# Rare blocks moved into open products, the next expert's rows fetched ahead of the overflow block, and one turn moved by six products

## The chip, the core and the metric

The kernel runs on one core of a Trainium2 chip. The metric is the device time of one execution in microseconds. The engines are PE (TensorE, matmuls and transposes through the array), DVE (VectorE), ACT (ScalarE), POOL (GpSimd) and SP (SyncE, which here issues the weight loads). Each engine works through its own queue in order, and engines wait for one another through semaphores.

## The reference

The reference is one layer of a graph network on N = 625 nodes with D = 1024 features and 20000 edges, all in float32:

```python
xn = _layernorm(x)
x = x + sage_twice(xn, src, dst) + linear_attention(xn)
x = x + moe(_layernorm(x))

# sage layer:   mean = segment_sum(h[src], dst) * deg_inv
#               h @ W_self + mean @ W_neigh + b          (relu between the two)
# attention:    softmax(q, over d) * 64**-0.5, softmax(k, over n); (q @ (k^T v)) @ Wo + bo   (16 heads of 64)
# moe:          softmax router over 8 experts, the best 2 of each node:
#               sum_k top_k * (silu(x @ w1[e_k]) @ w2[e_k])
#               + sigmoid(x @ sgw) * ((silu(x @ gate) * (x @ up)) @ sdown)
```

## The kernel before

**How a product is made.** Matmuls run on numbers split into a high half (a copy to float32r) and a low half (the rest), so that a product of x and w is three matmuls: high by high, high by low, low by high. A weight arrives in chunks of 128x1024 through a `Stream`: SP loads `wraw` (or `wmore`, further buffers in the expert stage), ACT casts it to `whi`, DVE subtracts to get `wlo` (both in the helper `split`, L99). There are three buffers each of `whi` and `wlo`, so the two engines run up to about two chunks ahead of PE. The stream's order is the order in which the weights were added at the start. `ts_half` (L201) is the product of all 625 rows by half of a weight's columns: four chunks `u`, in each of them five row tiles of six matmuls, into five banks of PSUM that stay open over the four chunks. A `step(u)` can be called after each chunk.

**The stages around the change, in order.** `psc` (L742) makes the attention context. Then comes the first rare block, `recount`, in a `tc.If(rare_v > 0)` (L748): it is for an adjacency count that does not fit the packed form, and with the inputs given it is not taken; the branch itself is executed by every engine. `psa` (L759) applies the context, `pso` (`ts_half` at L771) is the product with Wo, whose result is added to x on DVE and stored in DRAM (`accd`, L780) by POOL. `neighbours(xn)` (L783) is the first layer's product with W_neigh: `psg`, its tiles split into `g0h` and `g0l`. The second rare block (L793) follows, then `psag` (L819), the sums over neighbours. The second layer has the same form: `neighbours`, then `psx` (L847) with the self weights, added to `x2` (loaded back from `accd`, L851), the third rare block (L853), and `last_mean` (`psm`, L874), the sums over neighbours for the five tiles of rows in two groups, (0, 1, 2) and (3, 4). Where an If is not taken, an engine waits for its own work before it and then branches; an engine that needs a result or a buffer from another engine on the far side waits for that engine's branch.

**The second layer norm.** After a tile's means are complete, DVE adds them to `x2` and takes the statistics, ACT writes the normalised tile `xfn` (L273), and `turn` (L865) transposes it: eight PE transposes into two `pst` banks (L284), split by ACT and DVE into `xfh` and `xfl`. Tile 0 is turned inside tile 3's products, tiles 1 and 2 after tile 3, tile 3 and 4 inside the first products of the shared expert (`psga`, `psup`, L222).

**The experts.** Tokens are scattered by expert into `xsd`. Eight experts are taken by rank of load (`RANKS` = 0, 1, 2, 6, 3, 4, 5, 7), with room for 224, 224, 224, 128, 160, 160, 160, 128 rows in that order. Six are wide (`expert_wide`, L1178), two of 128 rows narrow. In a wide expert the first product (`pse`, L1196 and L1200) takes `xs`, the turned rows, through w1 in eight chunks; two `set` copies and additions (L1205, L1206), a silu and a split give `he`; the second product (`psy`, L1230 and L1253 to L1255) takes `he` through w2 in eight chunks, two halves of four; `y` is copied out and stored in `ysd` by POOL.

The rows of an expert come through a `Turn` (L1000). Making it issues the loads of `xb` on POOL (`expert_load`, L988; there is one buffer, so the turns of the expert before must have read it). Each `step()` finishes the turn before it (ACT copies the high half to `xs`, POOL subtracts the low half, both L99) and starts another: a 32x32 block transposition on DVE (`raw`, L1031). A wide expert has four turns. They are spread over the second product of the expert ahead:

```python
                if half or u > 1:
                    nxt().step()
...
                if aside and (half, u) == (0, 0):
                    aside(accs)
```

`aside` is `overflow` (L1292), for the first expert alone: a block for rows beyond an expert's room. It is not taken with these inputs. `nxt()` makes the Turn when it is first called.

## Time and profile before

| what | value |
|---|---|
| median of three runs | 1013.51 us (1012.4 to 1014.13) |
| the profiled execution | 1012.98 us |
| its span in the profile | 1011.4 us |
| PE busy | 996.1 us, 98%, 5541 instructions |
| DVE, ACT, POOL busy | 598.1, 395.3, 149.1 us |
| granted TensorE clock, mean over the span | 0.997 |

A time in the text such as "709" is in microseconds from the start of the span. In the list of waits, a line gives the engine, the tile it writes and the line of code, then what ended the wait, then the microseconds in total, how often, and the longest. In the chain of waits, the first two columns are start and length; "issue" is time in which the engine waits for nothing that the profile shows. In the table of windows, each engine has its busy time and number of instructions, then come the granted TensorE clock, the share of the DMA engines and GB/s. A releaser with a q (DVEq, PEq) is an engine's sequencer, here at a branch.

### The profile page before, as it was taken

What the parts mean: (1) busy time and instruction counts of PE and PEld (TensorE: products, weight loads), DVE (VectorE), ACT (ScalarE), POOL (GpSimd) and SP (SyncE); (2) the same over time, 40 slices, a digit from 0 to 9 for tenths busy, and PEclk for the clock granted to TensorE, in tenths of its full rate; (3) what the DMA queues carried; (4) which work ended last, traced back from release to release, by engine and by line L of the source; (5) the groups of instructions that cost most, each with busy time, mean ns of one, the idle gap of its engine ahead of it and who ended that gap; (6) DMA issues with size and microseconds to landing.
All of it is one profiled execution on the core that took longest, in us unless ns stands there. A gap on an engine that the chain in (4) does not pass through costs nothing. (4 is left out here: it accounts for less than half of the span.)

```text
span 1011.4 us, 14754 instructions
## 1 busy us (share of the span) xinstructions
PE 996.1 (98%) x5541; PEld 861.1 (85%) x5541; DVE 598.1 (59%) x1213; ACT 395.3 (39%) x577; POOL 149.1 (15%) x206
## 2 busy tenths in 40 slices
PE   9999999999999999999999999999899999999998
PEld 6999998888888888888878999997879787887886
DVE  7998745672523226333247264366777788887681
ACT  5534242231311122122116242264647576766610
POOL 1000011210145000200001003301332203120030
PEclk9999999999999999999999999999999999999999
DMA  8122237672234321412220226667877897887871
GB/s 243 53 64 67 81 117 257 229 246 73 96 122 155 124 84 43 143 63 83 84 63 3 64 63 208 204 188 228 238 240 238 276 348 248 282 299 252 333 257 53
DMA packets 111464, 164.67 MB, mean 163 GB/s; under 512 B 5931, under 2 KB 63443, under 8 KB 111382
## 3 DMA queue, kind: packets, MB, share of 16 engines
q1 hardware_dynamic: 97734, 118.38, 36.1%
q0 software_dynamic: 13456, 45.08, 13.6%
q8 instruction: 46, 0.75, 0.3%
q14 instruction: 36, 0.29, 0.1%
q10 hardware_dynamic: 192, 0.16, 0.0%
HBM read 133.19 MB, written 30.42 MB: 162 GB/s over the span
## 5 line engine op out<-in xcount | busy, mean ns | idle before, releaser
L99 DVE TENSOR_TENSOR wlo<-wraw,whi 128x1024 fp32r<-128x1024 f32 x148 | 186.4, 1260 | 249.1 <-ACT whi L99 244.8
L99 ACT CAST whi<-wraw 128x1024 fp32r<-128x1024 f32 x148 | 155.5, 1051 | 277.5 <-PE psg L212 66.2
L1200 PE MATMUL pse<-xs,whi 128*128 128x448 f32 (+1 forms) x384 | 110.9, 361 | 2.8 <-POOL xs L99 2.8
L99 DVE TENSOR_TENSOR wlo<-wmore,whi 128x1024 fp32r<-128x1024 f32 x67 | 82.2, 1227 | 28.2 <-ACT whi L99 27.0
L1196 PE MATMUL pse<-xs,wlo 128*128 128x224 f32 (+1 forms) x384 | 90.1, 255 | 0.0
L99 ACT CAST whi<-wmore 128x1024 fp32r<-128x1024 f32 x67 | 70.4, 1050 | 43.8 <-PE psz L212 17.0
L401 PE MATMUL psk<-xnh,whi 128*128 128x384 f32 (+3 forms) x240 | 74.5, 312 | 0.3 <-ACT xnh L99 0.3
L1200 PEld LDWEIGHTS pse<-xs,whi 128*128 128x128 f32 x384 | 69.9, 191 | 5.8 <-POOL xs L99 3.3
L402 PE MATMUL psk<-xnl,whi 128*128 128x384 f32 (+3 forms) x240 | 73.5, 306 | 0.6 <-DVE xnl L99 0.6
L403 PE MATMUL psk<-xnh,wlo 128*128 128x384 f32 (+3 forms) x240 | 73.5, 306 | 0.0
L1196 PEld LDWEIGHTS pse<-xs,wlo 128*128 128x128 f32 x384 | 72.8, 192 | 0.8
L1253 PE MATMUL psy<-whi,he 128*128 128x512 f32 (+1 forms) x176 | 69.5, 395 | 0.7 <-PEq L1295 0.7
L1254 PE MATMUL psy<-wlo,he 128*128 128x512 f32 (+1 forms) x176 | 69.6, 395 | 0.3 <-DVE wlo L99 0.2
L1255 PE MATMUL psy<-whi,he 128*128 128x512 f32 (+1 forms) x176 | 69.0, 392 | 0.0
L484 DVE TENSOR_SCALAR hot<-iota,srow,unit 125x128 f16<-125x128 f16 x160 | 49.4, 309 | 0.0
L402 PEld LDWEIGHTS psk<-xnl,whi 128*128 128x128 f32 x240 | 45.5, 190 | 0.8 <-DVE xnl L99 0.8
L401 PEld LDWEIGHTS psk<-xnh,whi 128*128 128x128 f32 x240 | 45.4, 190 | 0.6 <-ACT xnh L99 0.6
L403 PEld LDWEIGHTS psk<-xnh,wlo 128*128 128x128 f32 x240 | 45.4, 189 | 0.0
L99 POOL TENSOR_TENSOR xs<-raw,xs 128x512 fp32r<-128x512 f32 (+2 forms) x24 | 32.6, 1375 | 84.8 <-ACT xs L99 72.1
L483 DVE TENSOR_SCALAR hot<-iota,edt 125x128 f16<-125x128 f16 x160 | 39.6, 249 | 4.1 <-PE pa L501 4.1
L1253 PEld LDWEIGHTS psy<-whi,he 128*128 128x128 f32 (+1 forms) x176 | 31.9, 181 | 10.9 <-ACTq L1295 1.1
L1254 PEld LDWEIGHTS psy<-wlo,he 128*128 128x128 f32 (+1 forms) x176 | 31.8, 180 | 10.0 <-DVE wlo L99 1.6
(354 smaller groups left out, 2360.4 us busy)
## 6 DMA issues: line engine op xcount, KB each, us to landing
wraw<-in_L_ffn_w_dram SPq DMA_DIRECT2D x65, 512.0 KB, 5.3
wmore<-in_L_ffn_w_dram SPq DMA_DIRECT2D x63, 512.0 KB, 5.2
xsd<-zt POOLq DMA_DIRECT2D x9, 1024.0 KB, 5.5
wraw<-in_L_gnn_W_self_dram SPq DMA_DIRECT2D x16, 512.0 KB, 3.6
wraw<-in_L_gnn_W_neigh_dram SPq DMA_DIRECT2D x16, 512.0 KB, 3.7
wraw<-_ffn_shared_gate_up_dram SPq DMA_DIRECT2D x16, 512.0 KB, 3.9
wraw<-in_L_mix_Wk_dram SPq DMA_DIRECT2D x8, 512.0 KB, 6.1
wraw<-in_L_mix_Wq_dram SPq DMA_DIRECT2D x8, 512.0 KB, 3.7
```

The source lines that it names most:

```text
L99: return (order(nc.scalar.copy(hi, srcap)), order((eng or nc.vector).tensor_sub(lo, srcap, hi.bitcast(F32))))
L401: nc.tensor.matmul(ps[:, :n], wh[:, kt, :], xnh[:, kt, c], start=kt == 0, stop=False)
L402: nc.tensor.matmul(ps[:, :n], wh[:, kt, :], xnl[:, kt, c], start=False, stop=False)
L403: nc.tensor.matmul(ps[:, :n], wl[:, kt, :], xnh[:, kt, c], start=False, stop=kt == KT - 1)
L483: nc.vector.tensor_scalar(h[:ET, :WIN], iota[:ET, :WIN], edst[e], None, op0=ALU.is_equal)
L484: return nc.vector.tensor_scalar(h[:ET, WIN:], iota[:ET, :WIN], srow[e], unit[e].bitcast(F32), op0=ALU.is_equal, op1=ALU.mult)
L1196: nc.tensor.matmul(ps[a][:, :n], wl[:, k, c], xs[:, kt, 0, :], start=False, stop=False)
L1200: nc.tensor.matmul(ps[a][:, :2 * n], wh[:, k, c], xs[:, kt], start=kt == 0, stop=kt == KT - 1)
L1253: nc.tensor.matmul(acc, h(kt, 0), wh[:, k, :], start=kt == 0, stop=False)
L1254: nc.tensor.matmul(acc, h(kt, 0), wl[:, k, :], start=False, stop=False)
L1255: nc.tensor.matmul(acc, h(kt, 1), wh[:, k, :], start=False, stop=kt == KT - 1)
```

## The change

1. `neighbours(xn)` with its `psg` product is moved ahead of the first rare block; the weights' order changes with it (W_neigh of the first layer ahead of Wo).
2. The second rare block is called as a step inside `pso`, after the second chunk of the second half; the third is called in the same way inside `psx`. When taken, they use banks of their own. The loads of `x2` are issued ahead of the `psx` product.
3. In `last_mean`, tile 1 alone is turned after tile 3, and tile 2 inside tile 4's products, six matmuls later.
4. For the first expert too, the next expert's Turn is made before the expert's products; `nxt` is a Turn, not a function, and stepping begins with the second chunk of the second product (before: the third). The overflow block is called after the sixth chunk (before: after the first).
5. The overflow block's body is written smaller, as loops over halves of a weight, without the `Stream`, `Turn` and `expert_narrow` of before; their parameters for it are gone.

```diff
     add_ts(wv)
+    add_ts(wn0)
     add_ts(wo)
-    add_ts(wn0)
...
+    def hold(accs):
+        for t in range(NT):
+            nc.tensor.matmul(accs[t][rows(t), :128], zt[:, rows(t)], zt[:, :128], start=False, stop=False)
...
+    neighbours(xnh, xnl, g0h, g0l)
     rare_v = nc.values_load(rare[0:1, 0:1], min_val=0, max_val=2)
     with tc.If(rare_v > 0, preferred_fallthrough_block=False):
         recount()
...
+    def low_step(half, u, accs):
+        if (half, u) != (1, 1):
+            return
+        with tc.If(rare_v > 0, preferred_fallthrough_block=False):
...
+            hold(accs)
...
-        ts_half(aoh, aol, accs)
+        ts_half(aoh, aol, accs, step=lambda u: low_step(half, u, accs))
...
-    neighbours(xnh, xnl, g0h, g0l)
-    with tc.If(rare_v > 0, preferred_fallthrough_block=False):
...
+    def mean_low_step(half, u, accs):
+        if (half, u) != (1, 1):
+            return
+        with tc.If(rare_v > 0, preferred_fallthrough_block=False):
...
+            hold(accs)
     for half in range(2):
         accs = [bank("psx") for _ in range(NT)]
-        ts_half(hth, htl, accs)
+        for t in range(NT):
+            for r, q in pieces(t):
+                nc.gpsimd.dma_start(x2[q, t, hs], accd[r, hs])
+        ts_half(hth, htl, accs, step=lambda u: mean_low_step(half, u, accs))
         for t in range(NT):
-            for r, q in pieces(t):
-                nc.gpsimd.dma_start(x2[q, t, hs], accd[r, hs])
             nc.vector.tensor_add(x2[p, t, hs], accs[t][p, :], x2[p, t, hs])
-    with tc.If(rare_v > 0, preferred_fallthrough_block=False):
...
-                if (t, s) == (group[0], 2):
-                    turn(before)
+                if s == 2:
+                    turn(inside.get(t, ()))
...
-    last_mean((3, 4), (0,), {3: (1, 2)})
+    last_mean((3, 4), {3: (0,), 4: (2,)}, {3: (1,)})
...
+        nxt = nxt()
         for half in range(2):
             for u in range(4):
-                if half or u > 1:
-                    nxt().step()
+                if half or u:
+                    nxt.step()
...
-                if aside and (half, u) == (0, 0):
+                if aside and (half, u) == (1, 1):
                     aside(accs)
...
-        if i:
-            turn_of(i + 1)
-        expert_wide(first(r), CAPS[r], xs, turned[RANKS[i + 1]] if two else None,
-                    lambda: turn_of(i + 2 if two else i + 1), None if i else overflow)
+        nxt = turn(i + 1)
+        expert_wide(first(r), CAPS[r], xs, nxt if two else None,
+                    lambda: turn(i + 2) if two else nxt, None if i else overflow)
```

More of the change, by code (lines that the diff above doesn't have):

```diff
@@ L102, in gps_layer, with __init__ @@
     class Stream:
-        def __init__(self, ahead, pair=None):
-            self.pair, self.one, self.ready = pair, None, []
+        def __init__(self, ahead):
             self.todo, self.loaded, self.ahead, self.raw = [], 0, ahead, {}
@@ L116, in load @@
                     ap = self.todo[self.loaded] = ap()
-                if self.one is not None:
-                    r = self.one
-                elif self.more is not None and self.loaded % 2:
+                if self.more is not None and self.loaded % 2:
                     r = self.more.tile([128, D], F32, name="wmore", tag="wmore", bufs=MORE)
@@ L130, in next @@
         def next(self, eng=None, into=None, **order):
-            if self.ready:
-                return self.ready.pop(0)
             i = self.used
@@ L139, in next @@
                 hi, lo = into
-            elif self.pair is not None:
-                hi, lo = self.pair[:, i % 2, 0, :], self.pair[:, i % 2, 1, :]
             else:
@@ L745, in gps_layer, with neighbours @@
             nc.vector.tensor_scalar(cbd[r, o, r], ps[r, r], krs[r, o:o + 1], None, op0=ALU.mult)
+    def neighbours(xh, xl, gh, gl):
+        for half in range(2):
+            hs = slice(half * 512, (half + 1) * 512)
+            accs = [bank("psg") for _ in range(NT)]
+            ts_half(xh, xl, accs)
+            for t in range(NT):
+                split(accs[t][rows(t), :], gh[rows(t), t, hs], gl[rows(t), t, hs])
+    g0h, g0l = slot_n("g0h", F32R), slot_n("g0l", F32R)
+    neighbours(xnh, xnl, g0h, g0l)
     rare_v = nc.values_load(rare[0:1, 0:1], min_val=0, max_val=2)
@@ L751, in gps_layer @@
         inverse(NT - 1, 1)
+    def low_step(half, u, accs):
+        if (half, u) != (1, 1):
+            return
+        with tc.If(rare_v > 0, preferred_fallthrough_block=False):
+            for s in range(NT):
+                al = low_part(s)
+                for o in range(KT):
+                    for c0, n in PARTS:
+                        ps = bank("pslo")
+                        c = slice(c0, min(c0 + n, N))
+                        nc.tensor.matmul(ps[:, :n], g0h[rows(s), s, o * 128:(o + 1) * 128], al[rows(s), c0:c0 + n],
+                                         start=True, stop=True)
+                        lt = tmp.tile([128, NP], F32, name="lt", tag="tmp")
+                        nc.vector.tensor_mul(lt[:, c], ps[:, :min(n, N - c0)], dinv[:, c])
+                        nc.vector.tensor_add(hself[:, o, c], hself[:, o, c], lt[:, c])
+            hold(accs)
     aoh, aol = slot_t("aoh"), slot_t("aol")
@@ L780, in gps_layer @@
                 nc.gpsimd.dma_start(accd[r, hs], xr[q])
-    def neighbours(xh, xl, gh, gl):
-        for half in range(2):
-            hs = slice(half * 512, (half + 1) * 512)
-            accs = [bank("psg") for _ in range(NT)]
-            ts_half(xh, xl, accs)
-            for t in range(NT):
-                split(accs[t][rows(t), :], gh[rows(t), t, hs], gl[rows(t), t, hs])
-    g0h, g0l = slot_n("g0h", F32R), slot_n("g0l", F32R)
-    neighbours(xnh, xnl, g0h, g0l)
-    with tc.If(rare_v > 0, preferred_fallthrough_block=False):
-        for s in range(NT):
-            al = low_part(s)
-            for o in range(KT):
-                for c0, n in PARTS:
-                    ps = bank("pslo")
-                    c = slice(c0, min(c0 + n, N))
-                    nc.tensor.matmul(ps[:, :n], g0h[rows(s), s, o * 128:(o + 1) * 128], al[rows(s), c0:c0 + n],
-                                     start=True, stop=True)
-                    lt = tmp.tile([128, NP], F32, name="lt", tag="tmp")
-                    nc.vector.tensor_mul(lt[:, c], ps[:, :min(n, N - c0)], dinv[:, c])
-                    nc.vector.tensor_add(hself[:, o, c], hself[:, o, c], lt[:, c])
     hth, htl = slot_t("hth"), slot_t("htl")
@@ L843, in gps_layer @@
     x2 = slot_n("x2")
+    def mean_low_step(half, u, accs):
+        if (half, u) != (1, 1):
+            return
+        with tc.If(rare_v > 0, preferred_fallthrough_block=False):
+            for s in range(NT):
+                al = low_part(s)
+                for t in range(NT):
+                    for h in range(2):
+                        hs = slice(h * 512, (h + 1) * 512)
+                        ps = bank("pslo")
+                        p = rows(t)
+                        nc.tensor.matmul(ps[p, :], al[rows(s), cols(t)], g1h[rows(s), s, hs], start=True, stop=True)
+                        nc.vector.scalar_tensor_tensor(x2[p, t, hs], ps[p, :], degs[p, 2, t:t + 1], x2[p, t, hs],
+                                                       op0=ALU.mult, op1=ALU.add)
+            hold(accs)
     for half in range(2):
@@ L846, in gps_layer @@
         accs = [bank("psx") for _ in range(NT)]
-        ts_half(hth, htl, accs)
+        for t in range(NT):
+            for r, q in pieces(t):
+                nc.gpsimd.dma_start(x2[q, t, hs], accd[r, hs])
+        ts_half(hth, htl, accs, step=lambda u: mean_low_step(half, u, accs))
         for t in range(NT):
             p = rows(t)
-            for r, q in pieces(t):
-                nc.gpsimd.dma_start(x2[q, t, hs], accd[r, hs])
             nc.vector.tensor_add(x2[p, t, hs], accs[t][p, :], x2[p, t, hs])
-    with tc.If(rare_v > 0, preferred_fallthrough_block=False):
-        for s in range(NT):
-            al = low_part(s)
-            for t in range(NT):
-                for half in range(2):
-                    hs = slice(half * 512, (half + 1) * 512)
-                    ps = bank("pslo")
-                    p = rows(t)
-                    nc.tensor.matmul(ps[p, :], al[rows(s), cols(t)], g1h[rows(s), s, hs], start=True, stop=True)
-                    nc.vector.scalar_tensor_tensor(x2[p, t, hs], ps[p, :], degs[p, 2, t:t + 1], x2[p, t, hs],
-                                                   op0=ALU.mult, op1=ALU.add)
     xst = const.tile([128, NT, 2, 6], F32, name="xst")
@@ L867, in turn, with last_mean @@
             to_t(by_k(xfn[rows(t), t, :]), t, xfh, xfl, tc.keep_in_program_order)
-    def last_mean(group, before=(), after={}):
+    def last_mean(group, inside={}, after={}):
         accs = {t: [bank("psm") for _ in range(2)] for t in group}
@@ L1000, in gps_layer, with __init__ @@
     class Turn:
-        def __init__(self, row, n, into=None, bank=bank):
-            self.bank = bank
-            self.n, self.xb, self.xs, self.left = n, expert_load(row, n), into, None
+        def __init__(self, row, n):
+            self.n, self.xb, self.xs, self.left = n, expert_load(row, n), None, None
             self.todo = [(t0, g) for t0 in range(0, n // 32, 4) for g in range(2)]
@@ L1021, in step @@
             if n == 128:
-                ps = self.bank("psxt").rearrange("p (a b) -> p a b", b=128)
+                ps = bank("psxt").rearrange("p (a b) -> p a b", b=128)
                 for i in range(4):
@@ L1255, in rows_product, with expert_narrow @@
             nc.tensor.matmul(acc, h(kt, 1), wh[:, k, :], start=False, stop=kt == KT - 1)
-    def expert_narrow(row, xs, nxt, he=None, bank=bank):
-        if he is None:
-            he = big.tile([128, 2, KT, 128], F32R, name="he", tag="big")
+    def expert_narrow(row, xs):
+        he = big.tile([128, 2, KT, 128], F32R, name="he", tag="big")
         s = [None, None]
@@ L1270, in expert_narrow @@
             for u in range(4):
-                wh, wl = nxt()
+                wh, wl = st.next()
                 rows_product(acc, lambda kt, p: xs[:, p, kt], u, wh, wl)
@@ L1278, in expert_narrow @@
         for i, (half, u) in enumerate(TURNED):
-            wh, wl = nxt()
+            wh, wl = st.next()
             rows_product(accs[half], lambda kt, p: he[:, p, kt], u, wh, wl)
@@ L1284, in expert_narrow @@
             expert_out(row, accs[half:half + 1], half, nc.scalar.copy)
-    def turn_of(i):
-        r = RANKS[i]
-        if r not in turned:
-            turned[r] = Turn(first(r), CAPS[r])
-        return turned[r]
     def overflow(accs):
@@ L1298, in overflow @@
                 row = REG + j * 128
-                ovw = big.tile([128, 2, 2, D], F32R, name="ovw", tag="big")
-                ov = Stream(1, pair=ovw)
-                for w, aps in ((w1, row_aps), (w2, turned_aps)):
-                    for a in aps(w[ds(ej, 1)].rearrange("e k n -> (e k) n")):
-                        ov.add(a)
-                both = big.tile([128, 2, 2, KT, 128], F32R, name="both", tag="big")
-                banks = [bank(f"psov{i}") for i in range(4)]
-                count = {"psxt": 0, "psht": 0, "pse": 2, "psy": 2}
@@ L1308, in own @@
-                def own(name):
-                    count[name] += 1
-                    return banks[count[name] - 1]
-                turn = Turn(row, 128, both[:, 0], own)
-                ov.one = turn.xb[:, D:]
-                expert_narrow(row, turn.all(), ov.next, both[:, 1], own)
+                ovs = big.tile([128, 2, 2, D], F32R, name="ovs", tag="big")
+                xo = ovs[:, 0].rearrange("p a (k c) -> p a k c", c=128)
+                wh, wl = ovs[:, 1, 0].rearrange("p (a b) -> p a b", b=512), ovs[:, 1, 1].rearrange("p (a b) -> p a b", b=512)
@@ new lines, in overflow, with turn_all @@
+                turned_ps = [bank(f"psot{g}") for g in range(2)]
+                acc = bank("psov")
+                xb = expert_load(row, 128)
+                raw = xb[:, D:].rearrange("p (a b) -> p a b", b=512)
+                s = tmp.tile([128, 512], F32, name="set", tag="tmp")
+                def turn_all(src):
+                    for g, ps in enumerate(turned_ps):
+                        ps = ps.rearrange("p (a b) -> p a b", b=128)
+                        for k in range(4):
+                            nc.tensor.transpose(ps[:, k, :], src(4 * g + k), ident)
+                        split(ps, xo[:, 0, 4 * g:4 * g + 4, :], xo[:, 1, 4 * g:4 * g + 4, :])
@@ new lines, in product @@
+                def product(w, half):
+                    v = w[ds(ej, 1)].rearrange("e (k p) n -> (e p) k n", p=128)
+                    for u in range(4):
+                        nc.sync.dma_start(raw, v[:, 2 * u:2 * u + 2, ds(half * 512, 512)])
+                        split(raw, wh, wl)
+                        rows_product(acc, lambda kt, p: xo[:, p, kt], u, wh, wl)
+                turn_all(lambda kt: by_k(xb[:, :D])[:, kt])
+                with tc.For_i(0, 2, 1) as half:
+                    product(w1, half)
+                    nc.scalar.activation(s, acc, AF.Silu)
+                    nc.vector.tensor_copy(xb[:, ds(half * 512, 512)], s)
@@ L1315, in overflow, with turn @@
+                turn_all(lambda kt: xb[:, kt * 128:(kt + 1) * 128])
+                with tc.For_i(0, 2, 1) as half:
+                    product(w2, half)
+                    nc.scalar.copy(s, acc)
+                    nc.gpsimd.dma_start(ysd[ds(row, 128), ds(half * 512, 512)], s)
             for acc in accs:
                 nc.tensor.matmul(acc[:64, :128], zt[:, :64], zt[:, :128], start=False, stop=False)
+    def turn(i):
+        r = RANKS[i]
+        turned[r] = Turn(first(r), CAPS[r])
+        return turned[r]
@@ L1320, in gps_layer @@
         if r >= WIDE:
-            expert_narrow(first(r), xs, st.next)
+            expert_narrow(first(r), xs)
             continue
         two = i + 2 < NE and RANKS[i + 1] >= WIDE
-        if i:
-            turn_of(i + 1)
-        expert_wide(first(r), CAPS[r], xs, turned[RANKS[i + 1]] if two else None,
-                    lambda: turn_of(i + 2 if two else i + 1), None if i else overflow)
+        nxt = turn(i + 1)
+        expert_wide(first(r), CAPS[r], xs, nxt if two else None,
+                    lambda: turn(i + 2) if two else nxt, None if i else overflow)
     st.stop = None
```

## The prediction

> **What bounds the kernel now.** The page comes first. PE is busy for 996.1 of 1011.4 us and no other engine for more than 598.1, so the kernel is one stream of matmuls, and an edit that leaves the matmuls alone can only win what PE stands still. PE's own waits list nearly all of that:

> ```profile
> PE pse L1200 <- POOL xs L99: 2.8, 1, 2.8
> PE pswarm L248 <- DVE cold L245: 1.5, 1, 1.5
> PE psag L819 <- DVEq L793: 1.5, 1, 1.5
> PE pst L284 <- ACT xfn L273: 0.9, 1, 0.9
> PE psm L874 <- DVEq L853: 0.9, 1, 0.9
> PE psa L759 <- DVEq L748: 0.8, 1, 0.8
> PE psy L1253 <- PEq L1295: 0.7, 1, 0.7
> ```

> Six of the seven are places that the diff touches: the second expert's first product (L1200), the third tile's transposes (L284), three rare blocks (L748, L793, L853) and the overflow block (L1295). Below I price each by the step from the start of the matmul before the hole to the start of the one after, less the usual step; that counts refilling too: 2.96, 1.1, 0.99, 1.62, 1.03 and 0.84 us.

> The chain of waits says why the largest is there:

> ```profile
> 690.15 2.38 POOL xb L995 x4
> 692.53 13.94 issue
> 706.49 0.60 POOL ysd L1248
> 707.12 1.13 POOL xs L99
> ...
> 708.92 3.24 POOL xs L99 x2
> 712.16 0.04 issue
> 712.20 0.65 PE pse L1200
> ```

> The second expert's rows (xb) are fetched only behind the overflow block: among POOL's own waits `POOL xb L995 <- DVEq L1295` is 31.1 us. So DVE's turns and POOL's subtractions come late, and PE waits at 709 for the last low half.

> The windows around this hole show a second cost, the clock in the column after the five engines:

> ```profile
> 709.00:712.20 3.20, 0.40 (x2) 0.00 (x1) 3.20 (x3) 0.23 (x2) 3.15 (x2) 1.00 0.22 65
> 712.20:715.60 3.40, 3.40 (x12) 3.14 (x13) 3.36 (x4) 1.38 (x2) 3.17 (x5) 0.52 0.91 223
> 715.60:719.00 3.40, 3.40 (x23) 3.25 (x22) 1.38 (x2) 1.39 (x2) 1.45 (x3) 0.98 0.89 309
> ```

> For 3.40 us after the hole PE is granted half its clock: 12 matmuls in a time that then takes 23, so 11 x 0.148 = 1.63 us more are lost. After the holes of 0.8 to 1.6 us the clock stays full.

> **Part by part.** All sums are against the profiled execution: span 1011.4, time 1012.98, so 1.58 lie around the span; the median of the three runs, 1013.51, is 0.53 above it. I subtract the sum from the median.

> *The next expert's rows are fetched ahead* (`turn(i + 1)` for the first expert too, steps from the second chunk, overflow block after the sixth chunk). POOL issues the four loads when the first expert's turns have freed xb, near 657 instead of 690. An xb load lands after 4.2 to 10.7 us, so by 671, long before DVE's first turn (about 683). With one step per chunk of 12 x 0.2315 = 2.78 us the last of the four subtractions ends near 700, 9 us before the second expert needs it. Both costs of that hole go: -2.96 - 1.63 = -4.6 us. The block keeps its own price, 0.84: PE drains its own matmuls, branches (0.28) and refills, and no other engine is waited for. The next chunk's high and low halves stand ahead of the block on ACT and DVE, so the block does not hold them up. SP's branch waits for its transfers to land and so moves from 687 to about 699; the weight chunks from 689 to 698 land 2.7 to 11 us ahead of their casts with the xb loads among them (DMA share 1.06 from 695 to 705), and those loads leave this stretch for one at 0.55 (657 to 690), so I count a delay of about 2 us as hidden. Without that lead it would show in full, +2.

> *The third tile's turn, six products later.* PE stands 1.1 us at 540.98 because ACT writes xfn until 542.15. Six psm matmuls at 0.234 are 1.40 us, more than the hole, so it closes: -1.1. Next is the first psga matmul: the low halves of this tile then come up to 1.4 us later, about 0.3 ahead of need, so I keep a bound of +0.2.

> *The rare blocks.* Before, each stood between two stages, where DVE joins only after evicting the last tile: 0.99 + 1.62 + 1.03 = 3.64 us. After, `neighbours(xn)` stands ahead of the first block. There psa waits for DVE's branch behind the last g0l, the same situation as L793 before: 1.62. The bounds are 0.99 (the hole this block had) and 1.7. The other two come after two chunks of an open product, where the next chunk's halves stand ahead of the branch; the nearest row is the overflow block, also in an open product, 0.84 each; from below 0.64, the L793 time up to the end of the branch. The seams left without a block (pso to psag, psx to psm) start on banks evicted earlier, taken at nothing. One cover is thin: POOL's branch waits for half 0's accd stores to land, and the last x rows are loaded only behind PE's branch and two additions; xr loads land after 2.3 to 6.6 us. So the last POOL addition ends 0.3 to 4 us ahead of the sixth psag matmul, whose bank waits for it through a memset in DVE's queue: 0 to +0.7. Sum: 1.62 + 0.84 + 0.84 - 3.64 = -0.3 (from -1.4 to +0.7).

> *DVE's and ACT's order at the start of each wide expert's second product.* Starting one chunk earlier puts a second turn (1.15 to 1.2 us) between the two `set` additions, and for the 224-row experts two xs casts ahead of the second `set` copy. The trace of the second expert gives the lead:

> ```profile
> 735.85 0.39 DVE L1206 TENSOR_TENSOR set<-pse,set 128x224 f32<-128x224 f32 x1 [0.66 <-ACT set L1205]
> 736.80 1.23 DVE L99 TENSOR_TENSOR wlo<-wraw,whi 128x1024 fp32r<-128x1024 f32 x1 [0.56 <-ACT whi L99]
> 739.62 1.19 DVE L99 TENSOR_TENSOR wlo<-wmore,whi 128x1024 fp32r<-128x1024 f32 x1
> ```

> The wlo of 736.80 is ready at 738.03, and PE takes it at 739.74: 1.71 ahead; the next one likewise (740.81, 742.52). Turn, cast, copy and high half in the new order make them 1.45 and 1.25 later, so 0.26 and 0.46 stay. A POOL subtraction beside a wlo made it 1.71 instead of 1.23 (846.97), so a stall of up to 0.2 to 0.5 per 224-row expert is possible, two of them preparing a 224-row successor. In the 160-row experts the high half waits for the second copy anyway; there the second wlo moves ahead of its old place, behind a small turn (0.43) in place of one of 1.19, which closes their two holes of 0.2 (846.06, 881.27): -0.4. Together +0.1, from -0.4 to +2.

> [...]

> The rows go both ways: one wlo at 707.54 took 3.75 between two subtractions, but the one at 852.99 took 1.23 with POOL shown subtracting throughout. So I keep the 1.71.

> Sum: -4.6 - 1.1 - 0.3 + 0.1 = -5.9, taken as -6.0 with the rounding of the holes: a span near 1005.4, a time of 1013.5 - 6.0 = 1007.5 us.

> **Rivals.** *The low halves become the bound at the wide experts' second products* (the slower side). Five of these products turn a wide successor, and all now do it one chunk earlier. [...] It is slower by what can be measured from (6.0 + 2.0) / 5 = 1.6 us per expert. For it: 3.75 at 707.54, leads of 0.2 in the 160-row experts. Against: before, the same POOL work lay in the same products and cost 0.4 in all.

> *The weights cannot come faster.* From 806 to 832 and near 867 PE already follows the transfers, at a DMA share of 1.02 and 1.05. If what is won at 709 is waited for there, the -4.6 shrinks to about -1, all told -2 to -3: 1011. Against: a share of 0.79 and leads of 9 to 10 us from 740 to 795, which leaves room to rebuild a lead.

> *The hole stays*: the first expert's last turns still end late, or the block behind the sixth chunk breaks the lead and PE stands there and at half clock. Then -1.4 from the rest remains: 1012.1. Against it stand the 9 us worked out above.

> **From this to the numbers.** Forecast 1007.5, chance 0.66; weights 0.12; the hole stays 0.08; low halves late but netting a gain (about 1009.5) 0.04; the bound on low halves, slower, 0.10. About 0.2% (2.0 us) is what a measurement of this kernel can tell from no change. The hole that stays lies inside it, as does a small part of the weights' case: faster 0.80, same 0.10, slower 0.10. Range: below, all bounds at their good end, -1.4 and -0.4 in place of -0.3 and +0.1, and 1 us of scatter between runs: 1005.0. Above, the weights' case with scatter: 1012.0. Outside lie the slower case and half of the hole's.

> **What would show it.** Right: no wait of pse on xs near 709, and full clock there; no wait of pst on xfn; three short branch waits, two inside pso and psx near 0.84 and the first near 1.6; xb loads near 657. Wrong: waits of psy on wlo above 0.5 at the experts' second products, a window of half clock anywhere after the warm-up but the end, psag waiting for a late xr addition, or pse and psy waiting on whi through late weights.

## The result, and the profile after

The kernel after takes 1007.34 us (median of six runs, 1006.71 to 1007.66) against 1013.51 (1012.4 to 1014.55): a ratio of 0.9939, 95% interval 0.9927 to 0.9952, that is 4.9 to 7.4 us less. The forecast was 1007.5. Its profiled execution has a span of 1006.1 us, 5.3 below that of before, with the same 5541 PE instructions.

PE's own waits, as listed for the kernel before (engine, tile and line, releaser, us in total, times, longest):

```profile
PE psa L786 <- DVEq L757: 1.6, 1, 1.6
PE pswarm L246 <- DVE cold L243: 1.5, 1, 1.5
PE psy L1264 <- DVE wlo L99: 0.7, 2, 0.3
PE psy L1263 <- PEq L1298: 0.7, 1, 0.7
PE psk L400 <- DVE xnl L99: 0.6, 1, 0.6
PE psx L203 <- PEq L851: 0.5, 1, 0.5
PE pso L203 <- PEq L766: 0.5, 1, 0.5
PE psk L399 <- ACT xnh L99: 0.3, 1, 0.3
PE psa L786 <- DVE aol L99: 0.3, 1, 0.3
```

Gone are pse on xs (2.8), pst on xfn (0.9) and two waits for a branch of DVE's. In their place stand two waits of PE for its own branch (PEq) of 0.5. The first block still waits for DVE. Two lines are worse than before: psy on wlo, 0.7 against 0.2, and psa on aol, 0.3, which is new.

The windows where the second expert starts (busy time and number per engine, then the clock, DMA share, GB/s):

```profile
708.00:711.40 3.40, 3.40 (x22) 3.03 (x21) 3.02 (x4) 1.05 (x1) 1.72 (x3) 1.00 1.05 218
711.40:714.80 3.40, 3.40 (x24) 3.25 (x24) 1.90 (x3) 2.15 (x4) 0.00 (x0) 1.00 1.10 344
```

PE is never idle here and the clock is full. The timeline of POOL says why, its loads of xb and then the last two of the four subtractions (start, length, line, idle time before):

```profile
655.58 0.60 POOL L1005 DMA_DIRECT2D xb<-xsd  x1
657.15 1.78 POOL L1005 DMA_DIRECT2D xb<-xsd  x3
...
693.15 1.37 POOL L99 TENSOR_TENSOR xs<-raw,xs 128x384 fp32r<-128x384 f32 x1 [3.10 <-ACT xs L99]
699.42 1.35 POOL L99 TENSOR_TENSOR xs<-raw,xs 128x384 fp32r<-128x384 f32 x1 [0.64 <-ACT xs L99]
```

The loads go out at 656 to 659 (before: 690), and the last low half is ready at 700.8, 8.0 us before the second expert's first product at 708.8.

Where the 5.3 us of span went, from the start of the same stage in the two profiles:

| stage | before | after | difference | change of it |
|---|---|---|---|---|
| first transposes of x (start-up, outside the change) | 10.9 | 11.6 | +0.7 | +0.7 |
| psag (first block and pso's block ahead of it) | 386.6 | 387.7 | +1.1 | +0.4 |
| psm (third block) | 520.0 | 520.9 | +0.9 | -0.2 |
| psga (third tile's turn) | 547.4 | 546.9 | -0.5 | -1.4 |
| second expert, first product | 712.2 | 708.8 | -3.4 | -2.9 |
| second expert, second product | 734.0 | 728.9 | -5.1 | -1.7 |
| psz (the other experts) | 951.9 | 946.9 | -5.0 | +0.1 |
| end | 1011.4 | 1006.1 | -5.3 | -0.3 |

The start-up differs because the clock went to full at 5.77 us in the one execution and at 7.10 in the other. Without it the change is -6.0.

### The profile page after: what moved, and what is told of

Its sections match the earlier page's. It is cut to its first block, busy times and chain, and to the rows that moved or that the text cites. A ratio compares the mean times of both kernels' runs of the same rounds, so it can differ in the third digit from the quotient of the medians.

```text
span 1006.1 us, 14767 instructions
## 1 busy us (share of the span) xinstructions
PE 994.7 (99%) x5541; PEld 859.6 (85%) x5541; DVE 603.5 (60%) x1213; ACT 395.3 (39%) x577; POOL 143.5 (14%) x206
## 5 line engine op out<-in xcount | busy, mean ns | idle before, releaser
L99 DVE TENSOR_TENSOR wlo<-wraw,whi 128x1024 fp32r<-128x1024 f32 x148 | 189.2, 1279 | 245.9 <-ACT whi L99 241.9
L99 ACT CAST whi<-wraw 128x1024 fp32r<-128x1024 f32 x148 | 155.5, 1051 | 287.3 <-PE psg L205 75.1
L99 DVE TENSOR_TENSOR wlo<-wmore,whi 128x1024 fp32r<-128x1024 f32 x67 | 82.1, 1226 | 24.6 <-ACT whi L99 22.2
L1205 PE MATMUL pse<-xs,wlo 128*128 128x224 f32 (+1 forms) x384 | 89.5, 254 | 0.0
L99 ACT CAST whi<-wmore 128x1024 fp32r<-128x1024 f32 x67 | 70.4, 1051 | 41.1 <-PE psz L205 17.0
L1205 PEld LDWEIGHTS pse<-xs,wlo 128*128 128x128 f32 x384 | 72.0, 190 | 0.9
L99 POOL TENSOR_TENSOR xs<-raw,xs 128x512 fp32r<-128x512 f32 (+2 forms) x24 | 28.2, 1182 | 110.4 <-ACT xs L99 110.0
L1263 PEld LDWEIGHTS psy<-whi,he 128*128 128x128 f32 (+1 forms) x176 | 31.9, 181 | 10.9 <-issue 1.1
```

Of the source, the lines that this page charges most:

```text
L99: return (order(nc.scalar.copy(hi, srcap)), order((eng or nc.vector).tensor_sub(lo, srcap, hi.bitcast(F32))))
L1205: nc.tensor.matmul(ps[a][:, :n], wl[:, k, c], xs[:, kt, 0, :], start=False, stop=False)
L1263: nc.tensor.matmul(acc, h(kt, 0), wh[:, k, :], start=kt == 0, stop=False)
```

## The experiments

Each kernel ran beside the kernel before, whose medians lay between 1013.3 and 1013.4. Ratios are given with their 95% intervals; us are worked out from them with 1013.3.

### The three parts, one at a time

`p_fetch` is the kernel before with only the expert part:

```diff
+        nxt = nxt()
...
-                if half or u > 1:
-                    nxt().step()
+                if half or u:
+                    nxt.step()
...
-                if aside and (half, u) == (0, 0):
+                if aside and (half, u) == (1, 1):
...
+        nxt = turn(i + 1)
```

> The kernel before with only the expert part of the change: the next Turn made ahead for the first expert too, steps from the second chunk, the overflow block (in its small form) after the sixth chunk. Theory (each hole is its own and nothing ahead of it matters): the hole of 2.96 us at the second expert and the 1.63 us of half clock behind it go, the rest of the expert stage is as in the kernel after: a gain of 4.7 to 5.0 us, so about 1008.7 us, with no wait of pse on xs. Rival (the gain at the second expert needs the product that the rare blocks or the turn won ahead of it): a gain below 4 us. Rival (the weights' transfers give it back): a gain of 2 to 3 us with waits on whi from 800 on.

Measured: 1007.89, ratio 0.9946 (0.9934 to 0.9958), so -5.5 us (-6.7 to -4.3). No wait of pse on xs is left, and the clock is 1.00 from 700 to 714. The rivals with 2 to 4 us fall: this part alone carries nearly the whole change.

`p_turn` is the kernel before with only the third tile's turn moved:

```diff
-    last_mean((3, 4), (0,), {3: (1, 2)})
+    last_mean((3, 4), {3: (0,), 4: (2,)}, {3: (1,)})
```

> The kernel before with only the third tile's transposes moved six products later. Theory: 1.1 to 1.4 us less, 1012.1 to 1012.4, no wait of pst on xfn, psga unchanged. Rival (the wait moves on to psga, whose low halves come later): less than 0.5 us of gain and a wait of psga on xfl of 0.8 or more.

Measured: 1012.25, ratio 0.9987 (0.9979 to 0.9996), -1.3 us (-2.1 to -0.4). The wait of pst is gone and the one of psga is unchanged, 0.2 us each for xfh and xfl.

`p_rare` is the kernel before with only the rare blocks and the first `neighbours` moved:

```diff
+    neighbours(xnh, xnl, g0h, g0l)
     with tc.If(rare_v > 0, preferred_fallthrough_block=False):
         recount()
...
-        ts_half(aoh, aol, accs)
+        ts_half(aoh, aol, accs, step=lambda u: low_step(half, u, accs))
...
-        ts_half(hth, htl, accs)
+        ts_half(hth, htl, accs, step=lambda u: mean_low_step(half, u, accs))
```

> The kernel before with only the rare blocks and the first neighbours product moved. What was forecast: 0.3 us less, 1013.2, the first block at 1.6 and two at 0.84. From the trace of the kernel after: two blocks at 0.70, the first at 1.7, and a new hole of 0.45 inside psa, so 0 to 0.4 us more, 1013.5 to 1013.9. Rival (a block in an open product wins all that it cost at a seam, the first block none more): 1.3 us less, 1012.2.

Measured: 1013.04, ratio 0.9998 (0.9989 to 1.0007), -0.2 us (-1.1 to +0.7). From matmul to matmul the blocks cost 1.71, 0.71 and 0.71 and the new hole inside psa 0.35, together 3.48 against 3.64. This part does nothing that can be measured; the rival with 1.2 is out.

### Fetching ahead, or the block's place?

`a_bare0` is the kernel after with the overflow block at its old place:

```diff
-                if aside and (half, u) == (1, 1):
+                if aside and (half, u) == (0, 0):
                     aside(accs)
...
```

> The kernel after with the overflow block back behind the first chunk of the second product; the next Turn is still made ahead of the first expert's products. The block's taken path, which does not run with these inputs, is left out but for its closing matmuls, since with one xb buffer it could not stand ahead of the turns. Theory (what counts is that xb is asked for ahead of the block, not where the block stands): as the kernel after, 1007.3, xb loads near 657, no wait of pse on xs, the block's wait at 0.7 to 0.9 near 688. Rival (a block among the steps delays the turns, and the place behind the last step is what closes the hole): a wait of pse on xs of 1 us or more and 1008.5 or above.

Measured: 1006.83, ratio 0.9938 (0.9926 to 0.9950), as the kernel after. The xb loads go out from 654.3, no wait of pse on xs is left, and the block, with its body left out, costs 0.58 at 687. So what closes the hole is the loads' place ahead of the block in POOL's queue. The block's new place wins no time by itself. It is needed all the same: with the body kept at the old place (`a_aside0`) there is no result, because that kernel deadlocks; the body takes the one `xb` buffer, which by then holds rows whose turns come behind the block. The earlier start of the steps was not undone alone. By an estimate it is worth one chunk, 12 x 0.2315 = 2.8 us, of the 8.0 us of lead, so the hole would be closed without it.

### What a hole costs in clock

`d_hole8` and `d_hole11` open a hole of a chosen length at the same place, in the kernel after:

```diff
                 split(*self.left)
+                for _ in range(0 if self.todo else self.again):
+                    nc.gpsimd.tensor_sub(self.left[2], self.left[0], self.left[1].bitcast(F32))
...
         nxt = turn(i + 1)
+        nxt.again = 8 if i == 0 else 0
```

> The kernel after with the last low half of the second expert's xs subtracted nine times on POOL instead of once (the result is the same): a hole in PE ahead of the second expert that nothing else of the kernel before is needed for. Theory (POOL's end sets it): the 8 us of lead are used up, a wait of pse on xs of 0.5 to 2.5 us. On the clock: if a hole of this size is enough to halve it, PE is slow for 3.4 us or more behind it (1.6 us on top); if a hole has to fill most of a fixed window, the clock stays full.

> As the one before, with the last subtraction made twelve times: a hole three subtractions (3.3 to 4 us) longer, 4 to 6.5 us. Clock halved behind it for 3.4 us or more under every theory; the span then is longer than that of the kernel after by the hole and 1.6 us or more, less what the weights' lead gives back.

Measured: `PE pse L1212 <- POOL xs L1022` is 3.1 us with eight and 9.3 with eleven; from matmul to matmul, less the usual step, 3.30 and 9.41. The spans are 1009.2 and 1018.0, one execution each (1010.79 and 1019.61 us). The first hole is longer than expected because the eight further subtractions took 13.7 us, 1.71 each. The second is longer because the three further subtractions fall behind POOL's own branch at the overflow block and between the third expert's xb loads. The windows behind the two holes, `d_hole8` first:

```profile
713.90:717.30 3.40, 3.40 (x22) 3.25 (x23) 0.70 (x2) 1.03 (x3) 2.06 (x4) 1.00 0.67 214
```

```profile
719.60:723.00 3.40, 3.31 (x11) 3.09 (x12) 0.13 (x1) 0.35 (x1) 1.71 (x4) 0.50 0.63 174
```

A hole of 3.30 left the clock full. Yet the 2.96 of the kernel before had halved it for 3.4 us. The same hole, which `p_rare` and `p_turn` still have, settles how to read that. Behind it in `p_rare`, then in `p_turn`:

```profile
712.00:718.00 6.00, 6.00 (x21) 5.57 (x22) 3.35 (x5) 2.36 (x3) 4.61 (x7) 0.50 0.93 266
```

```profile
711.60:715.00 3.40, 3.10 (x19) 2.97 (x20) 3.40 (x5) 1.82 (x3) 3.13 (x6) 1.00 0.92 203
```

In `p_rare` the whole 6 us are at half clock: 21 matmuls in a time for 40, 2.9 us lost. In `p_turn` nothing is lost. So a hole near 3 us costs 0, 1.6 or 2.9 us more in these three executions.

In all twelve profiles of this case the granted clock changed only on a grid of 3.413 us, counted from the change to full clock at the start, which came between 4.7 and 7.4 us into the span. What the clock did behind these five holes goes with how much of the hole fell into one window of this grid (PE idle by the profile, in us):

| kernel | PE idle | windows, and the idle time in each | clock behind |
|---|---|---|---|
| `p_turn` | 709.11 to 711.90 | 707.17 to 710.58: 1.48; 710.58 to 713.99: 1.31 | full |
| `d_hole8` | 710.65 to 713.80 | 709.02 to 712.43: 1.78; 712.43 to 715.84: 1.37 | full |
| `p_rare` | 709.11 to 711.94 | 707.88 to 711.29: 2.17; 711.29 to 714.70: 0.65 | half, 711.29 to 718.12 |
| before | 709.40 to 712.20 | 708.92 to 712.33: 2.80 | half, 712.33 to 715.74 |
| `d_hole11` | 710.44 to 719.69 | 711.27 to 714.69: 3.41; 714.69 to 718.10: 3.41; 718.10 to 721.51: 1.59 | half, 714.69 to 724.93 |

Two of them window by window, PE alone (then clock, DMA share, GB/s), `p_turn` first:

```profile
707.17:710.58 3.41, 1.93 (x9) 1.00 0.67 229
710.58:713.99 3.41, 2.09 (x13) 1.00 0.51 156
713.99:717.41 3.42, 3.42 (x24) 1.00 0.78 159
```

```profile
707.88:711.29 3.41, 1.24 (x6) 1.00 0.24 77
711.29:714.70 3.41, 2.76 (x9) 0.50 0.76 199
714.70:718.12 3.42, 3.42 (x13) 0.50 0.91 282
718.12:721.53 3.41, 3.41 (x24) 1.00 1.02 285
```

Over the twelve profiles, from that change on, every window with 1.78 us of idle or less left the full clock as it was, and every one with 2.05 or more was followed by half clock. In the four profiles with half clock behind a hole, it ended only after a window without idle time; in `p_rare`, 0.65 us of idle kept it for a second window. So the second theory of `d_hole8`, that a hole has to fill most of a fixed window, is the one that fits. What is left to chance is where the grid falls, whose start differed from one execution to the next (4.7 to 7.4 us).

By the mean clock over the span, the kernel before paid in nearly every execution. The profiles without half clock behind a hole have 0.999 or 1.000, those with it 0.995 to 0.997. Of the 45 executions of the kernel before that ran beside these kernels, three have 0.999, and they are the shortest (spans of 1009.2 to 1009.6); the other 42 have 0.995 to 0.998 and 1010.4 to 1013.7.

### The low halves in the 160-row experts

`b_step` is the kernel after with the old start of the turns for these experts alone:

```diff
-                if half or u:
+                if half or u > beside:
                     nxt.step()
```

> The kernel after, but the 160-row experts begin the turns with the third chunk of the second product, as before; the 224-row experts keep the second chunk. Theory (in a 160-row expert the second turn's subtraction on POOL lies beside DVE's subtraction for he and stretches it from 0.56 to 1.55, and the low half behind it comes 0.5 late): two holes of 0.52 go back to 0.2, 0.6 us less than the kernel after, about 1006.7, he at 0.56. Rival (the holes come from the faster pace, with transfers or halves closer behind): no change, 1007.3, with holes of 0.5 at the same places.

Measured: 1006.62, ratio 0.9933 (0.9921 to 0.9946), 0.7 us below the median of the kernel after; the intervals of the two ratios overlap. The trace decides: the two holes go from 0.52 to 0.20 and 0.21. DVE's timeline in the kernel after, at the first of them:

```profile
836.95 1.30 DVE L99 TENSOR_TENSOR wlo<-wraw,whi 128x1024 fp32r<-128x1024 f32 x1 [0.30 <-ACT whi L99]
838.18 0.45 DVE L1040 STREAM_TRANSPOSE raw<-xb 128x128 f32<-128x128 f32 x1
838.56 1.55 DVE L1221 TENSOR_TENSOR he<-set,he 128x256 fp32r<-128x256 f32 x2
840.04 1.21 DVE L99 TENSOR_TENSOR wlo<-wmore,whi 128x1024 fp32r<-128x1024 f32 x1
```

And POOL's there:

```profile
837.88 2.15 POOL L99 TENSOR_TENSOR xs<-raw,xs 128x512 fp32r<-128x512 f32 x2 [0.70 <-ACT xs L99]
```

In `b_step` the same two subtractions take:

```profile
838.03 0.55 DVE L1221 TENSOR_TENSOR he<-set,he 128x256 fp32r<-128x256 f32 x2
```

The pair for `he` takes 0.55 us alone and 1.55 beside POOL's subtraction, ending at 840.11 as POOL ends at 840.03, and the wlo that PE waits for starts behind it. The wlo of 836.95 started beside POOL's subtraction before (835.86 to 837.18) and took 1.30, where the wlo of 832.84, with no POOL work beside it, took 1.23; so not every overlap costs as much.

### A further block in an open product

The trace of the kernel after leaves one block at a seam, the first (1.71, and the hole inside psa). `b_best` moves it into pso as well, on top of `b_step`:

```diff
+        if (half, u) == (0, 1):
+            with tc.If(rare_v > 0, preferred_fallthrough_block=False):
+                recount()
+                inverse(0, NT - 1)
+                inverse(NT - 1, 1)
+                hold(accs)
```

> The kernel after with the 160-row experts' turns from the third chunk, and the first rare block moved too, into the first half of pso behind its second chunk (with matmuls that keep the open banks, when taken). Theory (a block at a seam costs the wait for DVE's branch behind the last eviction, in an open product only PE's own drain, branch and refill): 1.71 and most of 0.33 inside psa go, 0.70 comes, so 1.0 to 1.3 us less than with the turns alone (1006.6): 1005.3 to 1005.6. Rival (psa now starts on banks that psg's last tiles still hold and waits for the same evictions without a branch): 0.3 us less or nothing, 1006.3 to 1006.6, with waits of psa on the last g0l or g0h of 1 us or more.

Measured: 1010.55, ratio 0.9973 (0.9962 to 0.9985): 3.9 us worse than `b_step`, which neither theory had. PE's waits and its branches at this line (PEldq is PE's sequencer; the lengths are shortest, median and longest, in ns):

```profile
PE pso L203 <- issue: 3.8, 1, 3.8
```

```profile
L761 PEldq COMPARE_BRANCH  x2: 98/1824/3549, 340.5 to 344.3; - x2
```

The hole is not a wait for another engine: one branch takes 3.55 us, and PE runs at a clock of 0.61 in the 3.4 us that follow. All of PE's branches in the kernels before and after take 0.06 to 0.32. Two kernels ask why:

```diff
         # b_small: recount without one of its loops (its taken path 124 PE instructions, not 177)
-        for t in range(NT):
-            pt = bank("psdt")
...
         # b_place: the whole body, one chunk earlier
-        if (half, u) == (0, 1):
+        if (half, u) == (0, 0):
```

> As b_best, the first rare block inside pso, but with its taken path, which does not run with these inputs, 53 PE instructions shorter (177 to 124; one loop of the recount is left out). In b_best PE's branch alone took 3.55 us against 0.3 of every other one. Theory (the branch waits for code: the way over the body is too long to be held ready): the branch at 0.3, the hole at 0.7 and no half clock, 1005.3 to 1005.6. Rival (it is the place in the stage, whatever the body): a branch of 3 us or more, 1010.5.

> As b_best with the whole body, but the first rare block one chunk earlier in pso (behind the first chunk). Theory (length of the body): a branch of 3 us or more again, 1010 to 1011. Rival (what counts is where the target falls in the code that is fetched piece by piece, which 30 matmuls fewer ahead of it shift): a branch of 0.3, 1005.3 to 1005.8.

Measured: `b_small` 1005.59, ratio 0.9926 (0.9914 to 0.9939); `b_place` 1005.76, ratio 0.9927 (0.9914 to 0.9939). In `b_place`:

```profile
L761 PEldq COMPARE_BRANCH  x2: 98/208/319, 332.5 to 336.3; - x2
```

The same body, jumped over from 30 matmuls earlier, costs 0.32 again, so its length alone is not the cause, and neither is a block inside pso as such. That the branch waits for code, and that where the target falls decides, is a guess that fits all three kernels. The traces have the packets of two instruction queues. In `b_best` one of 16 KB starts 0.9 us into the branch (345.22 to 346.33), and PE goes on 1.5 us after it. In `b_place` and `b_small` such a packet starts 1.0 us after the branch did, but PE has gone on by then. That `b_best` waited for this packet was not shown. Both kernels leave no wait of psa, the block costing 0.73 in all, and are the fastest seen: their runs (1005.1 to 1007.0 and 1005.0 to 1006.6) have medians 1.6 to 1.75 us below the kernel after, of which `b_step`'s part is 0.7; the intervals of the ratios overlap that of the kernel after. In `b_place` no part of the block is left out; its taken path does not run with these inputs.

## Why the prediction was right

The forecast of -6.0 came out at -6.2 by the medians. By its steps:

- *The rows fetched ahead, -4.6.* Right in place and mechanism: loads at 656, last subtraction at 700.8 ("near 700"), wait gone, clock full, and 4.6 between the two profiles (-2.9 and -1.7). The place of the overflow block had no part in it (`a_bare0`). What I took for a fixed price, 1.63 for the clock, is that of one execution; the same hole cost 0 and 2.9 in others. That the clock's part came out at 1.7 says little, since forecast and comparison start from the same execution of before. `p_fetch`, timed over six runs, gives 5.5 (4.3 to 6.7) for the part.
- *The overflow block's own price, 0.84.* Measured 0.85 at its new place.
- *The third tile's turn, -1.1.* -1.4 between the profiles, -1.3 (-2.1 to -0.4) alone. psga's waits stayed as they were, so the bound of +0.2 was not needed.
- *The rare blocks, -0.3.* Mis-sized in two terms that nearly cancel: the blocks in open products cost 0.70 and not 0.84 each, the first block 1.71 and not 1.62, and a hole of 0.45 inside psa was not in the sum: DVE makes a chunk's low half (326.51 to 327.74) before it reads psa's banks. Together +0.2 between the profiles, -0.2 (-1.1 to +0.7) alone. The thin cover held: POOL's last x addition ends at 384.6, 3.1 ahead of psag.
- *DVE's and ACT's order, +0.1.* The 224-row experts behaved as worked out, with no wait. In the 160-row experts the sign was wrong: the two holes were to close (-0.4) and grew from 0.2 to 0.52 (+0.6). The step that failed is that I put POOL's subtraction beside the wlo alone; it fell beside the `he` subtractions ahead of it, which took 1.55 in place of 0.56. The sum over the experts is +0.1 all the same, largely by luck: a hole of 0.38 in the narrow expert (820.8) went as well, which no term of the sum has and which is back in `b_best` (0.36 us of idle at 818.7).

Measured alone, the three parts add up to -7.0, inside the interval of the whole. Of the rivals, the bound on low halves did show itself, at 0.3 us in each of two experts where it needed 1.6 in five. The weights gave nothing back in the kernel after. `p_turn` gives a glimpse of that rival: in its profile, where no clock was lost at 709, PE waits 0.86 and 0.81 at 868 and 878, as much as the clock would have cost. The weights made them. ACT waits 2.3 us for a chunk whose load went out at 853.56 and landed 13 us later, and the chain of waits leads from there to the low halves that PE waits for at both places:

```profile
866.57 1.05 ACT L99 CAST whi<-wraw 128x1024 fp32r<-128x1024 f32 x1 [2.31 <-DMA wraw<-in_L_ffn_w_dram]
```

## What to carry to other kernels

Look at what stands in a queue ahead of a transfer, not only at when its data is needed: a branch on POOL between the request and its turn in the queue cost this kernel 2.96 us of matmuls and 1.6 in clock. What a hole of about 3 us cost in clock was not a fixed price (0, 1.6 and 2.9 us in three executions), so take it from many executions and not from one profile. A block that was not taken cost its drain, branch and refill (0.7 to 0.85 here) in the middle of an open product, and up to 1.71 at a seam where another engine had to evict first; but time each new place, since one branch took 3.55. When a POOL subtraction moves, list every DVE subtraction that it will lie beside, not only the one that the matmuls wait for: here two others took 1.55 us in place of 0.55.
